# A small-head attention block with two feed-forward parts on one core: loads of the first batch reordered, set-up products moved, one-column products taken off the matrix engine

## The chip, the cores and the metric

The kernel runs on one core of a Trainium2 chip. The core has five instruction streams that run side by side and wait for each other through semaphores: TensorE (matrix products and transposes, written PE in the profile, with its weight loads apart as PEld), VectorE (DVE), ScalarE (ACT), GpSimd (POOL) and SyncE (SP), which here only issues DMA transfers. The metric is the device time of one execution in microseconds; lower is better. The kernel before was measured three times: 1343.65, 1344.02 and 1346.45 us, median 1344.02.

## The reference

The input is x with 8 batches of 512 tokens and 256 features, in float32 throughout. Each of four sub-layers normalises x without a gain (`_layernorm`) and adds its result to x. Cut to what matters:

```python
x = x + attn_a(layernorm(x))   # 16 heads of 16, rope, latent kv of 64, softmax with a distance decay
x = x + ffn(layernorm(x))      # 256 -> 1024 -> 256, relu
x = x + attn_b(layernorm(x))   # (q k^T * decay) v over 256 features, no softmax
x = x + ffn(layernorm(x))      # the same weights again
```

`attn_a` also adds 0.2 * sigmoid(q . mean(k)) * mean(v) for each head, through the output weights. `attn_b` has q = x Wq^T + bq and k = x Wk^T + bk. Its scores are therefore x (Wq^T Wk) x^T plus terms in which a bias meets a weight (Wq^T bk, Wk^T bq) and one number, the sum of bq * bk. These three terms, which depend on weights alone, are what the kernel calls bb; the weight product is ct.

## The kernel before, in words

**Tiling.** Tokens lie on the 128 partitions in NT = 4 tiles of a batch. The 16 heads of `attn_a` are worked in NG = 4 groups of 4, each head on its own 32 partitions, so that products of 32 rows stand side by side in the array. One item is a token tile and a pair of heads; there are 8 items to a group, 32 to a batch and 256 in all (NS).

**The pass over items.** `score_item` makes scores s for an item, VectorE takes their row maxima (`reduce_item`, tile mr). After the 8 items of a group, `shift` turns the maxima (mx), negates them (neg) and sends them by a DMA on ScalarE's queue into spare rows of qT. Then `prob_item` makes the transposed products t with the maxima already taken off, ScalarE exponentiates them (p), VectorE or GpSimd multiplies them by the decay table dec_a, and `pv_item` multiplies them by the values. Probabilities lag scores by LAG = 10 steps.

**The rest of a batch** (output weights, the two feed-forward parts, `attn_b`) is cut into units, which a planner slips between the steps. It keeps a clock of its own for each engine, with estimated costs written into each unit (`pe`, `then`), and takes a unit when its inputs are due and its credit allows. All of this is done while the program is built: on the chip each engine has one fixed order.

**The start, which the change touches.** It is written out by hand. `move` (line 90 of the profile) issues DMAs on SP's queue in program order. SP has eight semaphores for them and takes them in turn, so a DMA is issued only when the one eight places ahead of it has landed. The loads before are, in order: x of batch 0 in two halves, vec (all bias columns), wd (the latent weights), wk_in, wq_in, rope, wv, two rows, wqk_in (the `attn_b` weights), one column of vec into its lower 64 partitions, x of batch 1, dec_a, two one-row loads into the gates (ga), and bvc. Then `stripes` copies the rotated q and k from SBUF to SBUF into qT and kT, four DMAs to a group of heads, and `late_loads` brings the output weights, wvu, w1, w2, dec_b, and a unit brings x of batch 2.

TensorE starts with 14 products of the identity with itself (`warm`), transposes the normalised x (tr_a), gathers the q and k biases (`biases`, tile qk_bias), and makes the latent in two halves (`latent(0, 2)`, `latent(1, 2)`), q and k for both rotary halves (`projected`), and the values. `regroup_k` and `regroup_q` are ScalarE copies that bring wk_in and wq_in into the order of the heads. The latent's evacuation by ScalarE adds the column of vec and sums over tokens into lsum.

**Set-up products.** `plain(0)` and `plain(1)` transpose the two `attn_b` weights with TensorE, `product(0)` and `product(1)` make ct from them. `product_biases` makes bb with TensorE from one-column products. `mean_v` makes the mean of the values from lsum, also with one column. Before, `plain(0)` stands ahead of the first scores; `plain(1)` and the two products are slipped in after score steps 1, 3 and 5, and `product_biases` is a planner unit that may start at step 20:

```python
    between = {
        1: Unit(lambda: plain(1), 700, (("ACT", 600),)),
        3: Unit(lambda: product(0), 900),
        5: Unit(lambda: product(1), 900, (("ACT", 600),)),
        9: ga0,
    }
```

In the profile nearly everything that VectorE, ScalarE and GpSimd do carries line 69, the wrapper that pins their order; products carry line 200 (`mm`) and transposes line 203 (`flip`). Operations are therefore told apart by their tiles.

Of the kernel before, what the change touches and what calls it, by code (L numbers as in the profile page):

```python
# [9 lines left out]
F32 = mybir.dt.float32  # L10
AF = mybir.ActivationFunctionType
ALU = mybir.AluOpType
# [3 lines left out]
P = 128  # L16
B, T, D = 8, 512, 256
NH, HD = 16, 16
HH = 8
# [3 lines left out]
LAT = 64  # L23
# [12 lines left out]
def tile_kernel(  # L36
# [41 lines left out]
    fr = ctx.enter_context(tc.tile_pool(name="fr", bufs=1))  # L78
    at = ctx.enter_context(tc.tile_pool(name="at", bufs=2))
    rs = ctx.enter_context(tc.tile_pool(name="rs", bufs=2))  # L80
    ps_sc = ctx.enter_context(tc.tile_pool(name="ps_sc", bufs=2, space=PSUM))
    ps_pv = ctx.enter_context(tc.tile_pool(name="ps_pv", bufs=1, space=PSUM))
    ps_m = ctx.enter_context(tc.tile_pool(name="ps_m", bufs=3, space=PSUM))
# [5 lines left out]
    def move(to, src):  # L89
        tc.keep_in_program_order(nc.sync.dma_start(to, src))  # L90
# [6 lines left out]
    def resident(src, name, shape=None):  # L97
        t = const.tile(list(shape or src.shape), F32, tag=name, name=name)
        move(t, src)
        return t  # L100
# [2 lines left out]
        return const.tile(shape, F32, tag=name, name=name)  # L103

    xs = {0: xp.tile([P, NT, D], F32, tag="x", name="x_0")}
    for h in range(2):
        move(xs[0][:, 2 * h : 2 * h + 2, :], xv[0][:, 2 * h : 2 * h + 2, :])
    ident = keep([P, P], "ident")
    make_identity(nc, ident)
    half = keep([P, NT], "half")  # L110
    gps.memset(half, -0.5)
    vec = resident(vecs, "vec")

    wd_sb = keep([P, NC, 2, LAT], "wd_sb")
    for j in range(2):
        move(wd_sb[:, :, j, :], wdown)

    wk_in = at.tile([P, NH, 32], F32, tag="p", bufs=4, name="wk_in")
    for j in range(2):
        move(wk_in[j * LAT : (j + 1) * LAT].rearrange("p h d -> p (h d)"), wk[:, 0, :])  # L120
    wq_in = at.tile([P, NC, NH, 32], F32, tag="p", bufs=4, name="wq_in")
    move(wq_in.rearrange("p c h d -> p c (h d)"), wq[:, :, 0, :])

    rope_sb = keep([P, 2, T], "rope_sb")
    move(rope_sb, rope[0:HH].unsqueeze(0).to_broadcast([NH, HH, 2, T]))
# [6 lines left out]
    wqk_in = rs.tile([P, NC, 2, D], F32, tag="big", bufs=1, name="wqk_in")  # L132
    move(wqk_in, wb[:, :, 0:2, :])
    bv, b2 = row[:, 0, :], row[:, 1, :]
    move(vec[LAT:, V_BD : V_BD + 1], vecs[:LAT, V_BD : V_BD + 1])

# [62 lines left out]
    def mm(o, l, r, start=True, stop=True):  # L199
        tc.keep_in_program_order(nc.tensor.matmul(o, lhsT=l, rhs=r, start=start, stop=stop))  # L200
# [24 lines left out]

    def regroup_q(e):
        for c in range(NC):
            act.copy(wq_sb[:, c, e, :].rearrange("p (h d) -> p h d", d=HH), wq_in[:, c, :, e * HH : (e + 1) * HH])


    qk_bias = keep([P, 2, 2], "qk_bias")
# [10 lines left out]
    def biases():  # L242
        ps = misc("qk_bias")
        for g in range(NG):
            for j, v in enumerate((V_BQ, V_BK)):
                for e in range(2):
                    mm(ps[g * 32 : g * 32 + 32, 2 * j + e : 2 * j + e + 1], pick[:, e, :], vec[:, v + g : v + g + 1])
        act.copy(qk_bias.rearrange("p j e -> p (j e)"), ps[:, :4])
# [29 lines left out]
        if c == NC - 1:  # L278
            act.copy(ct.rearrange("p c d -> p (c d)"), ps)

    def product_biases():
        both = rs.tile([P, NC], F32, tag="ve", name="both")
        dve.tensor_mul(both, vec[:, V_BQB : V_BQB + NC], vec[:, V_BKB : V_BKB + NC])
        ones = rs.tile([P, P], F32, tag="xn", name="ones")
        gps.memset(ones, 1.0)
        ps = misc("bb")
        for j, v in ((0, V_BKB), (1, V_BQB)):
            for c in range(NC):
                for o in range(NC):
                    mm(  # L290
                        ps[:, 2 * j + c : 2 * j + c + 1], wr[j][:, o, c * P : (c + 1) * P], vec[:, v + o : v + o + 1],
                        o == 0, o == NC - 1,
                    )
        for o in range(NC):
            mm(ps[:, 4:5], ones, both[:, o : o + 1], o == 0, o == NC - 1)
        dve.tensor_copy(bb, ps[:, :5])
        dve.tensor_copy(wvu[:, :, D], bb[:, 2:4])


    class Unit:  # L300
# [55 lines left out]
    def front1(b):  # L356
        def latent(part=0, parts=1):
            if part == 0:
                lat_a[b] = fr.tile([P, T], F32, tag="lat", name=f"lat_{b}")
                lsum[b] = fr.tile([P, parts], F32, tag="lsum", bufs=1, name=f"lsum_{b}")  # L360
            ps = misc(f"lat_{b}_{part}")
            n = T // parts
            cols = slice(part * n, (part + 1) * n)
            for c in range(NC):
                mm(ps[:, :n], wd_sb[:, c].rearrange("p j n -> p (j n)"), xT_a[b]["xT"][:, c, cols], c == 0, c == NC - 1)
            act.activation(
                lat_a[b][:, cols], ps[:, :n], AF.Identity,
                bias=vec[:, V_BD : V_BD + 1], accum_out=lsum[b][:, part : part + 1],
            )


        def values():
# [14 lines left out]


        def mean_v():
            ps = misc(f"mv_{b}")  # L390
            n = lsum[b].shape[1]
            for c in range(NC):
                for j in range(n):
                    mm(ps[:, c : c + 1], wv_sb[:LAT, c * P : (c + 1) * P], lsum[b][:LAT, j : j + 1], j == 0, j == n - 1)
            m = fr.tile([P, NC], F32, tag="mv_a", name=f"mv_a_{b}")
            dve.scalar_tensor_tensor(m, ps[:, :NC], 0.1 / T, bvc, ALU.mult, ALU.add)
            for c in range(NC):
                gps.tensor_scalar(vmean[:, c, : NH + 1], vmask[:, c, :], m[:, c : c + 1], None, ALU.mult)

        def through_wo():  # L400
            ps = misc(f"me_{b}")
            for c in range(NC):
                mm(ps[:, :D], vmean[:, c, :], wo_sb[:, c, :], c == 0, c == NC - 1)
# [359 lines left out]
    gps.memset(vaug[0], 1.0)  # L763
    memory_buffers()
    picks()
    warm(14)
    regroup_k()
    n0[0].fn(), n1[0].fn()
    n0[1].fn(), n1[1].fn()
    n0[2].fn()  # L770
    biases()
    regroup_q(0)
    latent(0, 2)
    masks()
    dve.memset(qT[0], 0.0)
    gps.memset(kT[1], 1.0)
    gps.memset(qT[1], 0.0)
    gps.memset(vaug[1], 1.0)
    loads_before_scores()
    n1[2].fn()  # L780
    latent(1, 2)
    regroup_q(1)
    half_unit(0, 0, projected(0, 0))
    k_ps = [projected(1, e) for e in range(2)]
# [7 lines left out]
            stripes(j, g, e)  # L792
    late_loads()
    order0[1].fn()
    plain(0)
    gps.tensor_scalar(bvc, bvc, 0.1, None, ALU.mult)
    order0[0].fn()

# [129 lines left out]
        u.done = 0  # L928
    ga0.after = []
    mv0.step = 12  # L930
    chains = [[mv0, me0, Unit(product_biases, 2400, (("DVE", 500),), step=20)], setup]
    for b in range(1, B):
        ln0, u1 = front1(b)
        ln0[0].step = ln0[3].step = max(LAG, PER * (b - 1) + 2)
# [2 lines left out]
    for b in range(B):  # L937
# [3 lines left out]
    tail_work = sum(u.pe for u in chains[-1]) + sum(u.pe for u in chains[-2][26:])  # L941


    between = {
        1: Unit(lambda: plain(1), 700, (("ACT", 600),)),
        3: Unit(lambda: product(0), 900),
        5: Unit(lambda: product(1), 900, (("ACT", 600),)),
        9: ga0,
    }
    for t in range(LAG):  # L950
        step(t)
        if t in between:
# [161 lines left out]
```

## Time and profile before

| what | value |
|---|---|
| median of three executions | 1344.02 us (1343.65 to 1346.45) |
| the profiled execution's own time | 1346.04 us |
| its span, first to last instruction | 1344.3 us |
| mean granted TensorE clock | 0.97 |
| TensorE busy | 1262.7 us (94%), 6152 instructions |
| VectorE busy | 808.9 us (60%) |
| ScalarE busy | 451.8 us (34%) |
| GpSimd busy | 402.1 us (30%) |
| SP's DMA queue | 18502 packets, 22.71 MB |

A row of the timeline gives the start in us, the time from there to the end of the last of the instructions merged into it, the engine, the line, the operation, what it writes and reads with partitions x elements, and how many instructions there are; in brackets stands how long the engine had been idle before it, and what released it. A float32 product appears as two matrix instructions. A clock of 0.50 means that TensorE was granted half speed.

### The profile page before, as it was taken

The numbers are of one execution on the slowest core, as the hardware profiler recorded it, in microseconds if no ns is written. First come the engines' busy times: TensorE is split into PE (matmuls) and PEld (weight loads), VectorE is DVE, ScalarE is ACT, GpSimd is POOL, SyncE is SP. The second block draws the span as 40 slices with busy tenths as digits, with TensorE's granted clock in tenths as the row PEclk, the third lists the DMA queues.
The fourth block names the chain that finished last, engine by engine and source line by source line (L and its number), as shares of the span: only waits on it lengthen the run. The fifth ranks groups of instructions, "written<-read, shape, count | busy, mean of one in ns | idle before, by whom it ended". The sixth has DMA issues, their size and how long they took to land. (4 is left out here: it accounts for less than half of the span.)

```text
span 1344.3 us, 15699 instructions
## 1 busy us (share of the span) xinstructions
PE 1262.7 (94%) x6152; PEld 628.0 (47%) x6152; DVE 808.9 (60%) x1324; ACT 451.8 (34%) x649; POOL 402.1 (30%) x459
## 2 busy tenths in 40 slices
PE   6999888989899999999999999999999899999988
PEld 3333233534354554453444544544554445455665
DVE  5667976657656775658756666657755575343130
ACT  2234434333434334324334334333333333331201
POOL 4145443233412432314232324214321232222010
PEclk8779989989899999999999999999999999998999
DMA  4300010001000010001000100001000000000000
GB/s 132 118 17 17 1 49 1 1 9 41 1 17 0 19 31 1 1 15 50 1 1 1 44 22 1 1 9 41 1 1 3 14 1 1 1 16 0 0 16 16
DMA packets 19215, 23.96 MB, mean 18 GB/s; under 512 B 4139, under 2 KB 13740, under 8 KB 18862
## 3 DMA queue, kind: packets, MB, share of 16 engines
q1 hardware_dynamic: 18502, 22.71, 5.7%
q8 instruction: 48, 0.79, 0.2%
q10 hardware_dynamic: 640, 0.26, 0.1%
q14 instruction: 25, 0.20, 0.0%
HBM read 10.11 MB, written 4.19 MB: 11 GB/s over the span
## 5 line engine op out<-in xcount | busy, mean ns | idle before, releaser
L69 DVE TENSOR_REDUCE mr<-s 128x2 f32<-128x1024 f32 x256 | 312.4, 1222 | 256.6 <-PE t L200 240.6
L69 ACT ACTIVATE p<-t 128x1024 f32<-128x1024 f32 (+1 forms) x290 | 264.2, 924 | 532.7 <-PE t L200 488.4
L69 POOL TENSOR_TENSOR p<-p,dec_a 128x512 f32<-128x512 f32 x182 | 231.9, 1295 | 508.4 <-ACT p L69 495.7
L200 PE MATMUL s<-kT,qT 32*128 32x512 f32 x1024 | 294.9, 664 | 49.4 <-DVE mr L69 45.9
L200 PE MATMUL t<-qT,kT 32*128 32x512 f32 x1024 | 301.7, 658 | 2.0 <-DMA qT<-neg 1.7
L69 DVE TENSOR_TENSOR p<-p,dec_a 128x512 f32<-128x512 f32 x330 | 226.3, 727 | 20.8 <-ACT p L69 20.8
L200 PE MATMUL x<-w_sb,h_x 128*128 128x256 f32 x1024 | 233.9, 383 | 0.0
L200 PEld LDWEIGHTS x<-w_sb,h_x 128*128 128x128 f32 x1024 | 190.4, 190 | 54.8 <-issue 30.1
L200 PEld LDWEIGHTS s<-kT,qT 32*128 32x128 f32 x1024 | 79.5, 189 | 220.0 <-DVE mr L69 99.3
L200 PE MATMUL pv<-p,va 128*32 128x512 f32 x1024 | 149.7, 621 | 1.4 <-DVE p L69 1.0
L69 ACT ACTIVATE h_x<-hx,vec 128x512 f32<-128x512 f32 x128 | 88.0, 688 | 152.0 <-PE hx L200 152.0
L200 PE MATMUL hx<-xT_f,w_sb 128*128 128x512 f32 x256 | 120.2, 609 | 0.7 <-ACT xT_f L69 0.7
L200 PE MATMUL hx<-xT_g,w_sb 128*128 128x512 f32 x256 | 119.4, 608 | 0.7 <-ACT xT_g L69 0.7
L69 DVE TENSOR_TENSOR x<-x,x 128x256 f32<-128x256 f32 x64 | 27.1, 423 | 148.5 <-PE x L200 148.5
L200 PEld LDWEIGHTS t<-qT,kT 32*128 32x128 f32 x1024 | 81.9, 187 | 17.7 <-issue 9.5
L200 PEld LDWEIGHTS hx<-xT_g,w_sb 128*128 128x128 f32 x256 | 46.8, 193 | 63.6 <-issue 58.5
L200 PEld LDWEIGHTS hx<-xT_f,w_sb 128*128 128x128 f32 x256 | 46.4, 193 | 58.4 <-issue 51.7
L200 PEld LDWEIGHTS pv<-p,va 128*32 128x32 f32 x1024 | 22.9, 109 | 77.6 <-issue 40.8
L69 POOL TENSOR_TENSOR x<-x,row 128x256 f32<-128x256 f32 x64 | 48.1, 771 | 32.9 <-DVE xn_f L69 22.3
L69 POOL TENSOR_TENSOR rc<-rc,rs 128x512 f32<-128x512 f32 x30 | 39.4, 1335 | 12.4 <-DVE rs L69 12.4
L200 PE MATMUL bs<-xT_r,ret 128*128 128x512 f32 (+3 forms) x128 | 38.0, 441 | 0.0
L200 PE MATMUL bo<-ret 128*128 128x256 f32 x160 | 36.6, 382 | 0.0
(137 smaller groups left out, 1037.3 us busy)
## 6 DMA issues: line engine op xcount, KB each, us to landing
kT<-rc SPq DMA_DIRECT2D x64, 64.0 KB
out_dram<-x SPq DMA_DIRECT2D x32, 128.0 KB
qT<-rc SPq DMA_DIRECT2D x60, 64.0 KB
x<-in_x_dram SPq DMA_DIRECT2D x7, 512.0 KB
w_sb<-in_w_dram SPq DMA_DIRECT2D x2, 1024.0 KB
x<-in_x_dram SPq DMA_DIRECT2D x2, 256.0 KB
wq_in<-in_wq_dram SPq DMA_DIRECT2D x1, 512.0 KB
rope_sb<-in_rope_dram SPq DMA_DIRECT2D x1, 512.0 KB
```

The costliest lines, as they stand in the source:

```text
L69: ins = f(*a, **k)
L200: tc.keep_in_program_order(nc.tensor.matmul(o, lhsT=l, rhs=r, start=start, stop=stop))
```

## The change

All of it lies in the first of the eight batches, or in terms made once from the weights.

- Loads: the one-column load into vec stands right behind the load of vec; wq_in stands ahead of wk_in. The two halves of x are written as two calls instead of a loop, in the same order.
- Start of TensorE: 7 warm products, the qk biases, 6 warm products; both pairs of transposes together; both halves of the latent together, later. The first `regroup_q` is done by VectorE instead of ScalarE, behind `masks` and ahead of the clearing of qT.
- `plain(0)`, `plain(1)`, `product(0)`, `product(1)` all stand ahead of the first scores. In their places after score steps 1, 3, 5 and 7 stand two warm products each.
- `product_biases` goes. `bias_rows` copies the two bias vectors to a small DRAM tile with a DMA that writes single elements, and reads them back as rows spread over all partitions. `bias_products`, after score steps 0, 2 and 4, multiplies the weights by these rows on GpSimd and sums along them with ScalarE's accumulator.
- The two halves of lsum are added by GpSimd when a latent is made in two parts, so that `mean_v` uses one column.

```diff
     vec = resident(vecs, "vec")
+    move(vec[LAT:, V_BD : V_BD + 1], vecs[:LAT, V_BD : V_BD + 1])
...
+    wq_in = at.tile([P, NC, NH, 32], F32, tag="p", bufs=4, name="wq_in")
+    move(wq_in.rearrange("p c h d -> p c (h d)"), wq[:, :, 0, :])
     wk_in = at.tile([P, NH, 32], F32, tag="p", bufs=4, name="wk_in")
     for j in range(2):
         move(wk_in[j * LAT : (j + 1) * LAT].rearrange("p h d -> p (h d)"), wk[:, 0, :])
-    wq_in = at.tile([P, NC, NH, 32], F32, tag="p", bufs=4, name="wq_in")
-    move(wq_in.rearrange("p c h d -> p c (h d)"), wq[:, :, 0, :])
...
-    move(vec[LAT:, V_BD : V_BD + 1], vecs[:LAT, V_BD : V_BD + 1])
...
-            act.copy(wq_sb[:, c, e, :].rearrange("p (h d) -> p h d", d=HH), wq_in[:, c, :, e * HH : (e + 1) * HH])
+            (act.copy if e else dve.tensor_copy)(wq_sb[:, c, e, :].rearrange("p (h d) -> p h d", d=HH), wq_in[:, c, :, e * HH : (e + 1) * HH])
...
-    def product_biases():
...
+    b_row = dr.tile([2, D], F32, name="b_row")
+
+    def bias_rows():
+        move(b_row.rearrange("j (c p) -> p (j c)", p=P), vecs[:, V_BQB : V_BQB + 2 * NC])
+        wr["rows"] = at.tile([P, 4, D], F32, tag="p", bufs=4, name="b_rows")
+        move(wr["rows"][:, 0:2, :], b_row.unsqueeze(0).to_broadcast([P, 2, D]))
+
+    def bias_products(j):
+        b_rows = wr["rows"]
+        w = b_rows[:, 2:4, :]
+        if j == 2:
+            gps.tensor_tensor(w[:, 0, :], b_rows[:, 0, :], b_rows[:, 1, :], ALU.mult)
+            act.activation(w[:, 0, :], w[:, 0, :], AF.Identity, accum_out=bb[:, 4:5])
+            act.copy(wvu[:, :, D], bb[:, 2:4])
+            return
+        gps.tensor_tensor(w, wqk_in[:, :, j, :], b_rows[:, 1 - j, :].unsqueeze(1).to_broadcast([P, NC, D]), ALU.mult)
+        for c in range(NC):
+            act.activation(w[:, c, :], w[:, c, :], AF.Identity, accum_out=bb[:, 2 * j + c : 2 * j + c + 1])
...
+            if part == 1:
+                gps.tensor_add(lsum[b][:, 0:1], lsum[b][:, 0:1], lsum[b][:, 1:2])
...
-                for j in range(n):
-                    mm(ps[:, c : c + 1], wv_sb[:LAT, c * P : (c + 1) * P], lsum[b][:LAT, j : j + 1], j == 0, j == n - 1)
+                mm(ps[:, c : c + 1], wv_sb[:LAT, c * P : (c + 1) * P], lsum[b][:LAT, 0:1])
...
-    warm(14)
+    warm(7)
+    biases()
+    warm(6)
     regroup_k()
     n0[0].fn(), n1[0].fn()
     n0[1].fn(), n1[1].fn()
-    n0[2].fn()
-    biases()
+    n0[2].fn(), n1[2].fn()
+    masks()
     regroup_q(0)
-    latent(0, 2)
-    masks()
     dve.memset(qT[0], 0.0)
     gps.memset(kT[1], 1.0)
     gps.memset(qT[1], 0.0)
     gps.memset(vaug[1], 1.0)
+    bias_rows()
     loads_before_scores()
-    n1[2].fn()
-    latent(1, 2)
+    latent(0, 2), latent(1, 2)
     regroup_q(1)
...
-    plain(0)
+    plain(0), plain(1), product(0), product(1)
...
-    chains = [[mv0, me0, Unit(product_biases, 2400, (("DVE", 500),), step=20)], setup]
+    chains = [[mv0, me0], setup]
...
-    between = {
-        1: Unit(lambda: plain(1), 700, (("ACT", 600),)),
-        3: Unit(lambda: product(0), 900),
-        5: Unit(lambda: product(1), 900, (("ACT", 600),)),
-        9: ga0,
-    }
+    between = {t: Unit(lambda: warm(2), 500) for t in (1, 3, 5, 7)}
+    between[9] = ga0
+    for j, t in enumerate((0, 2, 4)):
+        between[t] = Unit(lambda j=j: bias_products(j), then=(("POOL", 1300), ("ACT", 1300)))
```

In the built program the order of each engine beyond the first batch is the same as before. Within it, the planner also puts the two k products of batch 1 ahead of the transposes of the first group's result (num).

More of the change, by code (lines that the diff above doesn't have):

```diff
@@ L80, in tile_kernel @@
     rs = ctx.enter_context(tc.tile_pool(name="rs", bufs=2))
+    dr = ctx.enter_context(tc.tile_pool(name="dr", bufs=1, space=bass.MemoryType.DRAM))
     ps_sc = ctx.enter_context(tc.tile_pool(name="ps_sc", bufs=2, space=PSUM))
@@ L105, in tile_kernel @@
     xs = {0: xp.tile([P, NT, D], F32, tag="x", name="x_0")}
-    for h in range(2):
-        move(xs[0][:, 2 * h : 2 * h + 2, :], xv[0][:, 2 * h : 2 * h + 2, :])
+    move(xs[0][:, 0:2, :], xv[0][:, 0:2, :])
+    move(xs[0][:, 2:4, :], xv[0][:, 2:4, :])
     ident = keep([P, P], "ident")
@@ L279, in product @@
             act.copy(ct.rearrange("p c d -> p (c d)"), ps)
-    def product_biases():
[L282 to L297, printed above, removed]
+    b_row = dr.tile([2, D], F32, name="b_row")
[14 more added lines that the diff above has]
+            act.activation(w[:, c, :], w[:, c, :], AF.Identity, accum_out=bb[:, 2 * j + c : 2 * j + c + 1])
     class Unit:
@@ L359, in latent @@
                 lat_a[b] = fr.tile([P, T], F32, tag="lat", name=f"lat_{b}")
-                lsum[b] = fr.tile([P, parts], F32, tag="lsum", bufs=1, name=f"lsum_{b}")
+                lsum[b] = fr.tile([P, 2], F32, tag="lsum", bufs=1, name=f"lsum_{b}")
             ps = misc(f"lat_{b}_{part}")
@@ L390, in mean_v @@
             ps = misc(f"mv_{b}")
-            n = lsum[b].shape[1]
             for c in range(NC):
-                for j in range(n):
-                    mm(ps[:, c : c + 1], wv_sb[:LAT, c * P : (c + 1) * P], lsum[b][:LAT, j : j + 1], j == 0, j == n - 1)
+                mm(ps[:, c : c + 1], wv_sb[:LAT, c * P : (c + 1) * P], lsum[b][:LAT, 0:1])
             m = fr.tile([P, NC], F32, tag="mv_a", name=f"mv_a_{b}")
```

## The prediction

> **What bounds the kernel now.** I read the page first. TensorE is busy 94% of the span and the chain that ended last is nearly all TensorE, so after the start the order of its instructions carries time through: a lead won early is kept. The edits end with the product biases at about 85 us, so I then asked for the work by stage and for the timeline of the first 100 us. By stage (window, its length, busy us and count of TensorE, weight loads, VectorE, ScalarE, GpSimd; then TensorE clock, DMA share, GB/s):
>
> ```profile
> 9.50:15.90 6.40, 0.00 (x0) 0.00 (x0) 0.73 (x1) 1.54 (x5) 3.06 (x3) 0.90 1.06 316
> 15.90:21.50 5.60, 5.59 (x10) 2.70 (x12) 0.01 (x1) 0.95 (x4) 0.00 (x0) 0.50 0.06 14
> 30.90:46.00 15.10, 14.36 (x49) 5.83 (x49) 9.47 (x9) 1.17 (x2) 0.00 (x0) 0.66 0.50 151
> 80.80:98.40 17.60, 16.80 (x72) 7.12 (x68) 10.82 (x17) 4.99 (x9) 5.93 (x5) 0.61 0.08 20
> ```
>
> TensorE does nothing for 6.4 us, then runs at half clock; the first scores (30.9 to 46) and the stage with the product biases (80.8 to 98.4) are slow as well. The timeline names the waits:
>
> ```profile
> 6.36 0.30 ACT L69 COPY wk_sb<-wk_in 64x128 f32<-64x128 f32 x1 [4.01 <-DMA wk_in<-in_wk_dram]
> 9.19 0.61 SPq L90 DMA_DIRECT2D vec<-in_vecs_dram  x1
> 14.82 0.47 ACT L69 ACTIVATE lat<-lat,vec 128x256 f32<-128x256 f32 x1 [4.63 <-DMA vec<-in_vecs_dram]
> 15.91 2.08 PE L200 MATMUL lat<-xT_a,wd_sb 128*128 128x256 f32 x4 [6.41 <-ACT xT_a L69]
> 26.26 1.73 SPq L90 DMA_DIRECT2D kT<-rc  x2
> 30.88 1.33 PE L200 MATMUL s<-kT,qT 32*128 32x512 f32 x8 [3.31 <-DMA qT<-rc]
> 51.94 1.93 PE L200 MATMUL t<-qT,kT 32*128 32x512 f32 x6 [1.71 <-DMA qT<-neg]
> 56.45 1.86 PE L200 MATMUL mv<-lsum,wv_sb 64*128 64x1 f32 x8
> 80.77 1.95 PE L200 MATMUL bb<-vec,wr 128*128 128x1 f32 x16
> 83.52 0.98 PE L200 MATMUL bb<-both,ones 128*128 128x1 f32 x4 [0.80 <-DVE both L69]
> ```
>
> ScalarE waits 4.63 us for the second `vec` load, issued at 9.19 behind the large loads; the second `xT_a` copy and TensorE stand behind it. The first scores wait for the stripes of qT, the first t products for `neg`; mv and bb are one-column products that take TensorE time.
>
> **What the Trainium skill says.** *TensorE: Matmul & The Clock Gate*, Part 1 (the HAM clock gate): the clock is halved after a window of about 3.4 us without work and comes back after a busy one. The trace agrees: idle from 9.5, half at 14.8, full at 21.5; half again from 31.7 to 41.9, 52.4 to 62.2 and 82.9 to 96.7. *DMA: Bandwidth & Descriptors*, "Two DMAs through the same engine are not ordered": a DMA that touches what another one writes is issued only when the first one's semaphore has come. In before, nothing on SP's queue shows such a wait, as `vec` had long landed.
>
> **Part 1, the load order.** The second `vec` load now stands right behind the first and writes into the same tile, so SP must wait for the first to land. That was issued at 1.73. Least: 2.1 us after issue, as the stripe issued at 28.72 that releases 30.88, so 3.9; most 5.5; I take 4.7, since 512 KB of x lies ahead and its second half was used at 4.40. SP's own durations then give: vec until 5.3 (0.61), wd until 6.6 (1.31), wq until 7.2 (0.60), wk until 8.4 (1.25); every load behind is about 2.9 us later than before. x's 512 KB took 3.7 us from issue (0.72 to 4.40), wq took 4.8 (4.88 to 9.69, with wk ahead), so wq lands at 10.3 to 11.4, taken 10.5. wk is now behind it: about 11.4 instead of 6.97. ScalarE still has the wk_sb copies ahead of both xT copies. That is the new wait: wk_sb done at 11.7, xT at 12.3 and 12.9 (0.59 each), latents from 12.4. Both latents and the first q cost 1.1 + 1.1 + 2.0 at full clock (end 16.6) and 2.1 + 2.1 + 3.6 at half (20.2). At TensorE's start the qk biases now wait for `vec` (3.9 to 4.7, between 7 and 6 warm products), so the transposes come at 7.8 instead of 6.22 and end near 8.8; the wait for wk hides that (uncovered, 1.6). From 8.8 TensorE is idle, so the clock is open; I take 18.5 against 21.49 before: 3.0 us won (1.3 to 4.9), not the 6.4 that the old wait shows. The q copies moved to VectorE (two at about 0.3) and the 1.76 us memset behind them end near 13, before VectorE has other work; uncovered they would cost 0.6.
>
> **Part 2, the stripes.** From the first q to the first stripe is 4.77 us of VectorE and GpSimd (21.49 to 26.26), unchanged but for the lsum addition on GpSimd (about 0.25, in its 12.4 us of idle): 23.3. SP must be free by then. Two DMAs are new ahead of x_1, dec_a, two ga and bvc: b_row (512 pieces of 4 bytes to HBM) and b_rows, which reads it back and so waits for it. The old loads up to wqk were in by about 13.7, now 16.2; no row shows such a DMA, so b_row lands between 17.5 and, by an estimate from the same page's 0.2 us average HBM latency ("Latency and other measured facts") with 32 pieces on each of 16 engines and none overlapped, 16.2 + 6.4 + 2.1 = 24.7. I take 18.5; issuing b_rows to bvc takes 0.6 + 0.6 + 0.3 + 0.6 + 0.4, so SP is free at 21.0 and hides it (at the upper bound the stripes are 3.9 us late).
>
> **Part 3, plain and product ahead of the scores.** Four transposes, twice, and four ct products now stand before the first score. Their last bank waits for VectorE's va additions, which end 8.5 us after the first q (21.49 to 29.95): 27.0. Four products at 0.52 end at 29.1; the stripes would have let scores start at 23.3 + 4.6 = 27.9. So 1.2 us is given back: start 29.1 against 30.88.
>
> **Part 4, the first scores.** Before, 30.88 to the mx flip at 45.92, 15.0 us at clock 0.66 with wr and ct (1.11 + 2.08 + 1.75) between. Now TensorE comes in warm, and four pairs of warm products (28 instructions in 4.83, so 0.69 a pair) replace them. VectorE's eight reductions at 1.2 bound it: 1.4 + 9.6 + 1.0 for the pairs = 12.0, so mx at 41.1, 4.8 us earlier. The bias products fall here: GpSimd 1.3 + 1.3 + 0.8 (rows of 128x512 at 1295 ns, 128x256 at 771), ScalarE five at about 0.66 (lat's 475 + 192 ns) and a copy, 3.5. Both were nearly idle in this stage (0.00 and 1.17 us). On ScalarE they stand ahead of `neg`; uncovered they cost up to 3.5.
>
> **Part 5, neg.** It took 5.4 us from issue (46.54) to t (51.94), while w1 and w2 filled the DMA engines until 51. Those loads move only with the stripes (3.0). By latency t comes at 41.7 + 5.4 = 47.1, by the loads' end at 48.9; I take 48.0: 3.9 us won of the 4.8.
>
> **Part 6, one-column products.** mv halves: 0.9 us. bb leaves TensorE: 80.77 to 84.50, 3.7 us, with VectorE idle. The clock fell at 82.9, in bb, and stayed low until 96.7; if it stays up VectorE is next: reduction, p, four rope operations and the division end at 86.8 instead of 90.14 (3.3 won), and by 98 about 6.6 is won. I take 5.0.
>
> **Sum.** 3.9 + 0.9 + 5.0 = 9.8 us. The profiled execution took 1346.04 (span 1344.3) and would take 1336.2; the median lies 2.0 lower, so 1344.02 - 9.8 = **1334.2 us**.
>
> **Rivals.** *Front gain lost* (0.18): wk lands later, or b_row holds the stripes by 3 us; only part 6 is left, 1338. For: both waits are new and unmeasured; against: the loads have slack of some 2 us before the stripes. *Clock kept* (0.15): TensorE doesn't cool before the latents and neg isn't held by the weights; 4.9 instead of 3.0, all of part 6 (7.5) and 2 more: 13 to 17 won, 1329. For: the idle of 3.6 us is about one window; against: neg's 5.4 us under load. *Nothing measurable* (0.08): the clock falls elsewhere near 85 and the front gives nothing: 1344. *Slower* (0.09): the HBM round trip. ScalarE's five sums, and so `neg`, stand behind it, and so do the stripes. To cancel part 6 the first stripe must be issued 6 us later than before, near 32, so b_row must land after about 29.5, 13 us after its turn (0.4 us for each piece in line); after 20 us it is about 1351. For: no row shows its price; against: `vec`'s 64 small pieces landed with the stream around them.
>
> **Numbers.** The likeliest case (0.50) is 1331 to 1338. From 1327 to 1341.5 holds all but the last two cases and an edge. Faster by over 0.2% 0.83, within 0.2% 0.08, slower 0.09; 0.2% (2.7 us) is about what this measurement can tell from no change.
>
> **What would show it.** After: wk_sb waits for wk_in until about 11.4, latents at 12.4; a gap on SP before the second vec; first stripe at 23.3, scores at 29, mx at 41, t at 48; clock near 1.0 in the scores and around 85. Wrong would be: SP waiting for b_row beyond 21, t still at 52, or a clock fall where bb was.

## The result and the profile after

The changed kernel takes 1337.08 us (median of four runs, 1335.86 to 1339.7) against 1343.84 for the kernel before (1343.29 to 1346.45). The ratio is 0.9949, with a 95% interval of 0.9928 to 0.9969: 6.9 us less. The forecast was 1334.2, and its likeliest case ran from 1331 to 1338. The time is in it, at its slow end, but it did not get there by the way foretold. Medians and ratios leave out executions in a second, slower state, which concerns one of e2's seven (2435.72 us).

| | profiled, before | profiled, after |
|---|---|---|
| own time, us | 1346.04 | 1339.7 |
| span, us | 1344.3 | 1337.9 |
| mean clock | 0.970 | 0.977 |
| TensorE busy, us | 1262.7 | 1256.9 |

The work of the changed kernel by stage (window, its length, busy us and count of TensorE, weight loads, VectorE, ScalarE, GpSimd; then TensorE clock, DMA share, GB/s):

```profile
3.40:6.80 3.40, 2.98 (x48) 2.79 (x46) 2.60 (x11) 0.16 (x1) 3.10 (x11) 1.00 0.12 31
...
9.50:15.15 5.65, 0.00 (x0) 0.00 (x1) 1.99 (x3) 1.23 (x4) 3.04 (x3) 0.65 1.03 244
...
18.50:24.00 5.50, 4.91 (x14) 1.64 (x13) 3.63 (x6) 0.95 (x4) 0.36 (x2) 1.00 0.00 0
31.90:44.20 12.30, 11.62 (x56) 4.88 (x57) 9.92 (x9) 4.60 (x17) 3.88 (x5) 1.00 0.33 89
44.20:51.60 7.40, 3.70 (x12) 0.98 (x8) 4.06 (x7) 0.59 (x1) 0.94 (x2) 1.00 1.00 379
52.40:62.20 9.80, 9.80 (x37) 3.06 (x34) 4.53 (x7) 3.36 (x6) 5.66 (x6) 0.50 0.04 13
80.80:98.40 17.60, 17.12 (x66) 5.22 (x66) 13.35 (x19) 6.95 (x16) 9.02 (x8) 0.90 0.12 31
```

The first scores (31.9 to 44.2) now run at full clock and the stage that held bb (80.8 to 98.4) at 0.90 instead of 0.61: the first as foretold, the second with one fall of the clock left. But the DMA engines stand nearly idle from 3.4 to 6.8 and wholly from 18.5 to 24 (the second stretch was idle before as well, with SP waiting for the rotation), and the stretch from `neg` to the first t (44.2 to 51.6) has grown to 7.4 us, half of it idle for TensorE. Then 9.8 us at half clock follow, as before. The timeline (start, length, engine, line, operation, tiles, count, and in brackets the idle time and what ended it):

```profile
1.72 3.77 SPq L91 DMA_DIRECT2D vec<-in_vecs_dram  x2
...
12.79 0.36 DVE L69 COPY wq_sb<-wq_in 128x128 f32<-128x128 f32 x2 [4.71 <-DMA wq_in<-in_wq_dram]
13.66 0.62 SPq L91 DMA_DIRECT2D b_row<-in_vecs_dram  x1
13.66 0.30 ACT L69 COPY wk_sb<-wk_in 64x128 f32<-64x128 f32 x1 [7.59 <-DMA wk_in<-in_wk_dram]
...
15.15 3.40 PE L201 MATMUL lat<-xT_a,wd_sb 128*128 128x256 f32 x8 [6.87 <-ACT xT_a L69]
...
22.61 0.34 SPq L91 DMA_DIRECT2D b_rows<-b_row  x1
...
25.84 1.68 SPq L91 DMA_DIRECT2D kT<-rc  x2
...
28.45 3.58 PE L201 MATMUL ct<-wr 128*128 128x256 f32 x8 [0.68 <-ACT wr L69]
...
31.96 1.14 PE L201 MATMUL s<-kT,qT 32*128 32x512 f32 x8
...
42.68 1.06 SPq L91 DMA_DIRECT2D w_sb<-in_w_dram  x2
...
44.20 1.12 ACTq L69 DMA_DIRECT2D qT<-neg  x1
...
51.62 1.61 PE L201 MATMUL t<-qT,kT 32*128 32x512 f32 x6 [3.72 <-DMA qT<-neg]
```

Two new waits are plain. ScalarE waits 7.59 us for wk_in, and TensorE 6.87 us for what ScalarE does behind it. SP issues b_row at 13.66 and nothing more until 22.61. The waits of SP's queue (what it waited for: us in total, times, longest) give the wait for b_row its price, and that for the first load of vec:

```profile
SPq L91 <- DMA b_row<-in_vecs_dram: 8.2, 1, 8.2
SPq L91 <- DMA vec<-in_vecs_dram: 2.7, 1, 2.7
```

In the kernel before the last three events of the start stand so on the timeline, with the loads of w1 and w2 (`w_sb`) first:

```profile
41.27 1.07 SPq L90 DMA_DIRECT2D w_sb<-in_w_dram  x2
...
46.54 1.11 ACTq L69 DMA_DIRECT2D qT<-neg  x1
51.94 1.93 PE L200 MATMUL t<-qT,kT 32*128 32x512 f32 x6 [1.71 <-DMA qT<-neg]
```

So `neg` leaves 2.3 us earlier than before (44.20 against 46.54), the loads of w1 and w2 leave 1.4 us later (42.68 against 41.27), and t comes where it came before: 51.62 against 51.94.

Where the time went, from the starts of the same instructions in both profiles: t leads by 0.3 us, me of batch 0 by 0.7 (62.59 against 63.31), the first q of batch 1 by 4.85 (94.64 against 99.49), the first aT by 6.4 (116.75 against 123.19). At the last hx products it is still 6.5 (1320.2 against 1326.7), so all of it is made before 117 us. From the first aT to the end both take the same 1221.1 us.

### The profile page after: what moved, and what is told of

The parts are those of the page before. It is cut to its first block, busy times and chain, and to the rows that moved or that the text cites. A ratio compares the mean times of both kernels' runs of the same rounds, so it can differ in the third digit from the quotient of the medians.

```text
span 1337.9 us, 15694 instructions
## 1 busy us (share of the span) xinstructions
PE 1256.9 (94%) x6142; PEld 626.7 (47%) x6142; DVE 809.6 (61%) x1323; ACT 453.6 (34%) x658; POOL 405.0 (30%) x462
## 2 busy tenths in 40 slices
DMA packets 19887, 24.23 MB, mean 18 GB/s; under 512 B 4683, under 2 KB 14284, under 8 KB 19534
## 5 line engine op out<-in xcount | busy, mean ns | idle before, releaser
L201 PE MATMUL wo<-wo_sb,aT 128*128 128x256 f32 x128 | 36.2, 405 | 0.5 <-ACT aT L69 0.5
```

## The experiments

Each ran beside the kernel before; 1343.9, 1342.94 and 1342.96 us were its medians in the three groups (e1 to e4, e5 to e8, e9 to e12). Ratios are to it; the ratio on record is not the quotient of the two medians, and the two differ by up to 0.0013. Gains in us with an interval are worked out from the ratio. In e2 to e8 and in e12 the two bias vectors lie as rows in the input data, so that one broadcast load fetches them and no trip is needed.

**e1: the front alone.** The changed kernel, with bb on TensorE again; the trip and its rows stay, unused.

```diff
-    def bias_products(j):
...
+    def product_biases():
...
-    chains = [[mv0, me0], setup]
+    chains = [[mv0, me0, Unit(product_biases, 2400, (("DVE", 500),), step=20)], setup]
...
-    for j, t in enumerate((0, 2, 4)):
-        between[t] = Unit(lambda j=j: bias_products(j), then=(("POOL", 1300), ("ACT", 1300)))
```

> Everything of the change stays, with the b_row round trip and its loads, but the product biases are made by TensorE again, at the old place. Theory A (all of the gain comes from bb leaving TensorE; the front gives nothing): first t near 51.6 as after the change, bb again about 3.7 us, the clock falls in it, and the time is that of before less 0.3 to 1 us: 1343, ratio 0.999 to 1.000. Rival B (the front carries a good part of the gain and bb's 4 us are given back later): 1340 or less, ratio 0.997 or less.

Measured: 1340.89 us, ratio 0.9974 (0.9963 to 0.9986), between the two forecasts; the interval reaches Rival B's 0.997 but not Theory A's 0.999. The starts of me of batch 0 and of the first q of batch 1, in the kernel before, the changed kernel and e1:

```profile
63.31 1.13 PE L200 MATMUL me<-wo_sb,vmean 128*128 128x256 f32 x4
99.49 1.98 PE L200 MATMUL q<-xT_a,wq_sb 128*128 128x512 f32 x4
```

```profile
62.59 1.13 PE L201 MATMUL me<-wo_sb,vmean 128*128 128x256 f32 x4
94.64 1.98 PE L201 MATMUL q<-xT_a,wq_sb 128*128 128x512 f32 x4
```

```profile
60.56 1.13 PE L201 MATMUL me<-wo_sb,vmean 128*128 128x256 f32 x4
96.74 1.98 PE L201 MATMUL q<-xT_a,wq_sb 128*128 128x512 f32 x4
```

From one to the other e1 takes 36.18 us, exactly what the kernel before takes; the changed kernel takes 32.05. By these profiles bb's share is 4.1 us. The front is not worth nothing: 3.5 us (1.9 to 5.0) with mv.

**e2: bb and mv alone.** The kernel before, with one column for mv and bb made by GpSimd and ScalarE after score steps 2, 4 and 6.

```diff
-    chains = [[mv0, me0, Unit(product_biases, 2400, (("DVE", 500),), step=20)], setup]
+    chains = [[mv0, me0], setup]
...
+    for j, t in enumerate((2, 4, 6)):
+        between[t] = Unit(lambda j=j: bias_products(j), then=(("POOL", 1300), ("ACT", 1300)))
```

> The kernel before, with nothing but the one-column products changed: mv from one column, bb by GpSimd and ScalarE after score steps 2, 4 and 6. The two bias vectors come as rows in one load from the laid-out inputs, so there is no round trip through HBM. Theory A: all of the gain, first t near 52, no clock fall where bb was, 1337 to 1338.5, ratio 0.995 to 0.996. Rival B: half of it, 1341, ratio 0.998.

Measured: 1339.07 us, ratio 0.9957 (0.9938 to 0.9975), 5.8 us less by the ratio and 4.8 by the medians. The first q of batch 1 comes at 96.67, 2.8 us earlier than before although t was 1.1 us later (53.01). The ratio by itself is the one that Theory A named. The gains of e1 and e2 add up to more (9.3) than the changed kernel has (6.9), within their intervals; mv's shorter products are in both. Theory A (all from bb) falls in its strict form, by e1. That bb is the larger part is the likelier reading, but the intervals of the two gains overlap.

**e3: no trip.** The changed kernel, with one load of the rows in place of b_row and b_rows.

```diff
-        move(b_row.rearrange("j (c p) -> p (j c)", p=P), vecs[:, V_BQB : V_BQB + 2 * NC])
...
-        move(wr["rows"][:, 0:2, :], b_row.unsqueeze(0).to_broadcast([P, 2, D]))
+        move(wr["rows"][:, 0:2, :].rearrange("p j d -> p (j d)"), rows[3 * D : 5 * D].partition_broadcast(P))
```

> The changed kernel without the round trip: the bias rows come in one load from the laid-out inputs; all else as changed. SP no longer waits 8.2 us. Theory C (the trip alone lost the front gain): stripes from 25 at full pace, first scores at 29.5 instead of 31.96, first t 2.5 us earlier, 1334.5. Rival D (the first scores wait as much for ct, which ended at 32.03, and the first t for the end of the weights' loads): scores still at 31 to 32, first t 1 to 1.5 us earlier as SP is done earlier, 1335.5 to 1336.5.

Measured: 1334.75 us, ratio 0.9931 (0.9911 to 0.9950), which overlaps that of the changed kernel; the profiled execution (1338.59) was the slowest of six. Its timeline shows why taking an 8.2 us wait away won so little:

```profile
26.10 1.72 SPq L90 DMA_DIRECT2D kT<-rc  x2
...
29.41 1.99 PE L200 MATMUL ct<-wr 128*128 128x256 f32 x8 [0.68 <-ACT wr L69]
...
31.34 1.14 PE L200 MATMUL s<-kT,qT 32*128 32x512 f32 x8
```

The first stripe leaves at 26.10, no earlier than with the trip (25.84): q starts at 18.33, as late as before the edit, and SP now waits 8.3 us for the rotation instead of b_row. The time is the one that Theory C (the trip alone) named, but not its way: the scores start at 31.34 and t is 1.0 us earlier (50.58), which is what Rival D said.

**e4: the weight products back among the scores.** e3 with `plain(1)`, `product(0)` and `product(1)` after score steps 1, 3 and 5 and no warm pairs.

```diff
-    plain(0), plain(1), product(0), product(1)
+    plain(0)
...
-    between = {t: Unit(lambda: warm(2), 500) for t in (1, 3, 5, 7)}
-    between[9] = ga0
+    between = {
+        1: Unit(lambda: plain(1), 700, (("ACT", 600),)),
+        3: Unit(lambda: product(0), 900),
+        5: Unit(lambda: product(1), 900, (("ACT", 600),)),
+        9: ga0,
+    }
```

> As the run without the round trip, but plain(1) and the two ct products stand among the scores again, where they were before the change, in place of the warm products. Rival D: first scores 2 us earlier than with ct ahead (29.5), but the scores take 13 to 15 us instead of 11.6, so mx comes no earlier (43 to 44) and the time is the same within 1 us. Theory C: no difference in the first scores.

Measured: 1337.32 us, ratio 0.9944 (0.9928 to 0.9961), not separated from e3, though its median is 2.6 us above. The scores start at 29.60, waiting for a stripe, but take 15.4 us to mx (44.98), at a mean clock of 0.67, instead of 11.6; mx is 2.0 us later than in e3, and t comes at 51.17 against 50.58. What the place of the products gives at one end of the scores it takes at the other, and t hardly moves either way. That is the way of Rival D; whether its time (within 1 us of e3) holds, the intervals can't tell.

**e5: wk first.** e3 with wk_in ahead of wq_in, as in the kernel before.

```diff
-    move(wq_in.rearrange("p c h d -> p c (h d)"), wq[:, :, 0, :])
...
     for j in range(2):
         move(wk_in[j * LAT : (j + 1) * LAT].rearrange("p h d -> p (h d)"), wk[:, 0, :])
...
+    move(wq_in.rearrange("p c h d -> p c (h d)"), wq[:, :, 0, :])
```

> This is e3 (no round trip) with the key weights loaded ahead of the query weights again, as in the kernel before. Theory W (the late key weights hold the latents in the changed kernel and that is what reaches the first t): wk_sb comes at about 9 us instead of 13.7, the latents start at about 10 to 11 instead of 14.75 and the first q at about 13 to 15 (it now waits for the query weights, about 12.8), the first stripe is issued at about 22 instead of 26.1, first scores at about 27, and the first t at 47 to 48 instead of 50.6, since the loads of w1 and w2 move with the stripes: 1331 to 1333 against 1334.75 for e3. Rival X (the wait only changes its name: the query weights, the rope and the clock then bind): latents earlier, but q at 17 to 18, first stripe at 25 or later, t at 50 and 1334 to 1335.

Measured: 1331.54 us, ratio 0.9912 (0.9899 to 0.9925).

```profile
10.89 1.99 PE L200 MATMUL lat<-xT_a,wd_sb 128*128 128x256 f32 x8 [0.74 <-ACT xT_a L69]
...
20.60 1.72 SPq L90 DMA_DIRECT2D kT<-rc  x2
...
44.51 2.10 PE L200 MATMUL t<-qT,kT 32*128 32x512 f32 x6 [2.73 <-DMA qT<-neg]
```

With q at 13.79 and the first scores at 25.84 this is Theory W, at each step as early as expected or earlier.

**e6: the vec column later.** e5 with the one-column load behind wk_in.

```diff
-    move(vec[LAT:, V_BD : V_BD + 1], vecs[:LAT, V_BD : V_BD + 1])
...
         move(wk_in[j * LAT : (j + 1) * LAT].rearrange("p h d -> p (h d)"), wk[:, 0, :])
+    move(vec[LAT:, V_BD : V_BD + 1], vecs[:LAT, V_BD : V_BD + 1])
```

> This is e5 with the one-column load of vec behind the key weights, so that SP no longer waits 2.7 us for the first load of vec. Theory V (this wait delays every later load): all loads behind are issued 2.7 us earlier, wk_sb at about 7.5, query weights about 10, the first q at about 11 to 13, the first stripe at about 20, t at about 45 to 46, and about 2 us less time than e5. Rival Y: the loads share the bandwidth, so what is issued earlier lands no earlier by more than 1 us, or the column itself is then late and holds the latents and the bias of q; time within 1 us of e5.

Measured: 1329.28 us, ratio 0.9889 (0.9873 to 0.9906). The wait is gone, and the timeline reads:

```profile
8.25 1.99 PE L200 MATMUL lat<-xT_a,wd_sb 128*128 128x256 f32 x8
...
18.81 1.71 SPq L90 DMA_DIRECT2D kT<-rc  x2
...
22.13 3.57 PE L200 MATMUL ct<-wr 128*128 128x256 f32 x8 [0.68 <-ACT wr L69]
25.63 1.14 PE L200 MATMUL s<-kT,qT 32*128 32x512 f32 x8
```

The latents come 2.6 us earlier than in e5 and the stripe 1.8, but the scores only 0.2: ct stands ahead of them and fell into a stretch of half clock (3.57 us against 1.99 in e5). t is 0.9 us earlier (43.57). The step from e5 alone isn't separated by the intervals; from e3 to e6, both load edits together, it is.

**e9: the trip kept, the load order mended.** The changed kernel with the load order of e6.

```diff
-    move(vec[LAT:, V_BD : V_BD + 1], vecs[:LAT, V_BD : V_BD + 1])
...
-    move(wq_in.rearrange("p c h d -> p c (h d)"), wq[:, :, 0, :])
...
         move(wk_in[j * LAT : (j + 1) * LAT].rearrange("p h d -> p (h d)"), wk[:, 0, :])
+    move(vec[LAT:, V_BD : V_BD + 1], vecs[:LAT, V_BD : V_BD + 1])
...
+    move(wq_in.rearrange("p c h d -> p c (h d)"), wq[:, :, 0, :])
```

> This is the changed kernel with the trip through HBM kept, and only the load order of e6: key weights ahead of the query weights, the one-column load of vec behind the key weights. Theory L (the two new waits in the loads cost the changed kernel its front gain, with or without the trip): the trip starts 3 us earlier with the loads, b_row is issued at about 10 to 11 and lands at about 19, its rows at about 25, the stripes go out from about 20.5 to 22, first scores at 26 to 27, first t at 45 to 46, and 1330 to 1332 against 1337.1 for the changed kernel. Rival T (the trip binds the stripes as soon as the loads are mended, so it is what decides): SP stays held to 22 or later, first scores at 29 or later, t at 48 or later, 1333 to 1336.

Measured: 1336.83 us, ratio 0.9955 (0.9944 to 0.9967): nothing won on the changed kernel. SP's waits, the timeline and a stretch of the scores:

```profile
SPq L91 <- DMA b_row<-in_vecs_dram: 9.5, 1, 9.5
```

```profile
20.05 0.34 SPq L91 DMA_DIRECT2D b_rows<-b_row  x1
...
22.91 3.68 PE L201 MATMUL ct<-wr 128*128 128x256 f32 x8 [0.67 <-ACT wr L69]
23.16 1.82 SPq L91 DMA_DIRECT2D kT<-rc  x2
...
29.18 1.53 PE L201 MATMUL s<-kT,qT 32*128 32x512 f32 x8 [2.58 <-DMA qT<-rc]
```

```profile
34.20:37.60 3.40, 3.40 (x16) 1.68 (x12) 2.28 (x2) 0.59 (x3) 0.11 (x1) 0.50 0.41 104
```

q now starts at 12.78 instead of 18.39, 5.6 us earlier, but SP sits on b_row until 20.05, the x, dec_a, ga and bvc loads go after it, and the stripes after those. The scores wait for a stripe, the clock falls, and mx comes at 43.58, where the changed kernel has it (43.59). That is Rival T, though b_row landed 2 us sooner than it said. Together with e3 and e6 this makes a square:

| | load order of the change | load order of e6 |
|---|---|---|
| with the trip | 1337.08, ratio 0.9949 (first scores 31.96) | 1336.83, 0.9955 (29.18) |
| without the trip | 1334.75, 0.9931 (31.34) | 1329.28, 0.9889 (25.63) |

The late weights and the trip stand side by side ahead of the same stripes. Either alone holds the scores; removing one wins 2.3 us at most, removing both wins 7.8, and only e6's interval stands apart from the other three.

**e10: w1 and w2 early, on the kernel before.** The only edit:

```diff
         move(bvc, rows[0:D].rearrange("(c p) -> p c", p=P))
+        late["w1"] = resident(w1, "w1_sb")
+        late["w2"] = resident(w2, "w2_sb")
...
-        late["w1"] = resident(w1, "w1_sb")
-        late["w2"] = resident(w2, "w2_sb")
```

> This is the kernel before with one edit: w1 and w2 (2 MB) issued behind bvc, ahead of the stripes. Theory N (these loads fill the DMA engines while neg's 8 KB are on the way): from the issue of neg to the first t about 3.5 us instead of 5.4, so t about 2 us earlier than 51.9 and the time 1.5 to 2 us below the kernel before. Rival Q (the stripes, behind 2 MB on the same queue, come later): first scores at 32 or later instead of 30.9, and a time equal or longer.

Measured: 1337.89 us, ratio 0.9971 (0.9959 to 0.9983): 3.9 us less by the ratio, 5.1 by the medians. From `neg` to t it takes 2.6 us, and TensorE is at work all the while:

```profile
48.17 1.12 ACTq L69 DMA_DIRECT2D qT<-neg  x1
...
50.75 0.70 PE L200 MATMUL t<-qT,kT 32*128 32x512 f32 x2
```

The first scores came at 31.98, as Rival Q had it, so t is only 1.2 us earlier than before; yet me of batch 0 is 4.9 earlier (58.38 against 63.31). The rest is the clock. The same stretch of both kernels, before first:

```profile
52.40:62.20 9.80, 9.80 (x40) 3.87 (x34) 4.47 (x7) 3.37 (x6) 4.28 (x5) 0.50 0.00 0
```

```profile
52.40:62.20 9.80, 9.06 (x52) 3.94 (x50) 9.43 (x14) 5.08 (x10) 5.62 (x6) 1.00 0.01 3
```

Without the idle time ahead of t the clock doesn't fall: 52 products instead of 40 in 9.8 us. From t to me takes 7.6 us here and 11.4 in the kernel before. The wait for `neg` was paid twice, once as idle time and, for 3.8 us, as half clock behind it. The other profiles say the same. In the five without idle time ahead of t (e7, e8, e10, e11, e12) it is 7.6 us from t to me; in the other nine, with 1.7 to 3.7 us of idle time, it is 9.7 to 11.4.

**e7: w1 and w2 early, on e6.** The edit of e10.

> This is e6 with the loads of w1 and w2 (2 MB) issued on SP's queue ahead of the stripes, right behind bvc, instead of behind the first stripes. Theory N (neg takes 7.4 us because these loads fill the DMA engines): from the issue of neg to the first t 2.5 to 3.5 us instead of 7.4, so t about 4 us earlier after mx. Rival Q (the stripes then stand in line behind 2 MB, about 11 us at 190 GB/s): the first scores come 5 us or more later than in e6, at the end t is no earlier or later, and the time is 0 to 5 us above e6.

Measured: 1325.1 us, ratio 0.9858 (0.9840 to 0.9875), the fastest kernel of the study, 18 to 19 us below the kernel before and 12 below the changed one. Its interval just overlaps that of e6.

```profile
37.12 1.12 ACTq L69 DMA_DIRECT2D qT<-neg  x1
...
40.83 1.15 PE L200 MATMUL t<-qT,kT 32*128 32x512 f32 x6
```

```profile
37.60:41.00 3.40, 3.39 (x13) 1.15 (x14) 2.49 (x7) 0.59 (x1) 0.83 (x2) 1.00 0.54 184
```

From `neg` to t 3.7 us instead of 5.7 in e6 (37.87 to 43.57), TensorE busy all the while and the clock at 1.00; from t to me 7.6. The stripes lose nothing (scores at 24.88), because the 2 MB fill a stretch in which e6 leaves the DMA engines more than half idle (share 0.39 and 0.35 from 17.0 to 20.4 and 23.8, against 1.05 and 0.83). Theory N holds, though 3.7 us is a little over the 2.5 to 3.5 expected, and Rival Q falls here.

**e8: the products back, on e7.** The edit of e4.

> This is e7 with plain(1) and both weight products among the first scores again, in the places of the warm pairs. If the stripes bind the first scores in e7 (Rival Q), the products ahead of the scores cost nothing there and moving them back makes this kernel 2 to 4 us slower than e7; if the products bind (Theory D: first scores stand right behind ct), the scores start 2 to 3.5 us earlier, and take 3 us longer, so that the time is within 1.5 us of e7.

Measured: 1328.58 us, ratio 0.9884 (0.9865 to 0.9903). The scores start at 25.22, waiting for a stripe, and take 15.6 us (mx 40.80), at a mean clock of 0.64, instead of 11.6: 3.5 us slower than e7, in Rival Q's range, though the two intervals overlap a little.

**e11: the trip back, on e7.** The edit of e3 turned round: b_row and b_rows in place of the one load.

> This is e7 with the trip through HBM put back, which shows the price of the trip where the other waits are gone, with w1 and w2 then issued behind the rows that are read back. Theory T: SP is held for b_row some 8 us, w1 and w2 leave at about 24 and fill the engines in front of and beside the stripes, so first scores at 28 to 30 instead of 24.9 and t at 45 to 47 instead of 40.8: 1329 to 1332 against 1325.1. Rival (the trip is covered by the latents and the rotation, as the prediction had it): within 1.5 us of e7.

Measured: 1338.7 us, ratio 0.9966 (0.9953 to 0.9980), 14 us slower than e7.

```profile
19.92 0.34 SPq L91 DMA_DIRECT2D b_rows<-b_row  x1
...
22.82 1.65 SPq L91 DMA_DIRECT2D w_sb<-in_w_dram  x2
25.29 2.18 SPq L91 DMA_DIRECT2D kT<-rc  x2
...
33.88 2.09 PE L201 MATMUL s<-kT,qT 32*128 32x512 f32 x8 [9.67 <-DMA qT<-rc]
```

w1 and w2 now leave right ahead of the stripes, and TensorE waits 9.67 us for a stripe behind them. Worse than Theory T: the trip doesn't only delay, it throws the large loads onto the stripes. Its 22 executions spread from 1333.45 to 1344.37, and the profiled one took 1334.88, so the profiles of e7 and e11 differ by about 10 us and not by 14; what makes the spread stays open.

**e12: no warm pairs, on e7.**

```diff
-    between = {t: Unit(lambda: warm(2), 500) for t in (1, 3, 5, 7)}
-    between[9] = ga0
+    between = {9: ga0}
```

> This is e7 without the four pairs of warm products among the first scores. The prediction priced the pairs at 1.0 us in this stage. If they only fill TensorE's waits for VectorE's reductions, removing them gains nothing: first scores to mx stays at 11.6 us, and t and time within 1 us of e7. If they stand in the way, mx comes 1 us earlier and the time is 1 us less. If they hold the clock up, the clock falls in the scores, and the scores, the t and the time are 2 us or more later than in e7.

Measured: 1328.97 us, ratio 0.9909 (0.9888 to 0.9931), 4 us slower than e7 and with an interval apart from e7's. The same stretch of the scores, e7 first, then e12:

```profile
30.80:34.20 3.40, 3.40 (x18) 1.42 (x16) 2.83 (x4) 1.50 (x7) 0.93 (x2) 1.00 0.27 77
```

```profile
30.80:34.20 3.40, 3.21 (x12) 1.01 (x8) 2.36 (x2) 0.79 (x5) 0.60 (x1) 0.50 0.21 67
```

The third branch came: without the pairs the clock falls and the scores take 13.7 us (23.93 to 37.66) instead of 11.6, and t is 2.2 us later (43.05). The pairs cost nothing that shows here; they hold the clock. The two profiled executions hide it in their totals (1324.55 and 1324.85): e12 is 1.6 us behind at the first aT (105.78 against 104.16) and wins most of that back behind it.

## Why the prediction was right or wrong

The sum was 3.9 (t earlier) + 0.9 (mv) + 5.0 (bb) = 9.8 us. The two profiled executions differ by 6.3. By the starts of their instructions the front and mv together gave 0.7, bb 4.1 and a stretch of half clock that is gone 1.6. That the time lies in the likeliest case is in part luck: the last 1.6 us stand in no term of the sum, and without them the time would, as an estimate, be near 1339, outside that case.

| step | predicted | measured |
|---|---|---|
| Part 1: SP's wait for the first vec; vec issued until | 5.3 | 5.49 |
| wq in use | 10.5 | 12.79 |
| wk in use (second half) | 11.4 | 14.19 (first half 13.66) |
| latents | 12.4 | 15.15 |
| first rotation after q | 18.5 | 20.37 |
| Part 2: b_row landed | 18.5 (17.5 to 24.7) | 22.6 |
| first stripe | 23.3 | 25.84 |
| Part 3: four ct products | 2.1 long | 3.58 |
| first scores | 29.1 | 31.96 |
| Part 4: first scores to mx | 12.0 long | 11.6 |
| mx | 41.1 | 43.59 |
| Part 5: `neg` issued to t | 6.3 long (5.4 to 7.2) | 7.4 |
| t | 48.0 | 51.62 |
| Part 6: mv | 0.9 won | 0.85 (1.86 to 1.01 long) |
| bb | 5.0 won | 4.1 |

**Part 1: mechanism right, size wrong.** SP did wait for the first vec, 2.7 us. With the second vec's own issue behind it the loads moved by 3.3 us (wd from 2.23 to 5.54), and wk behind wq became the new wait. The term mis-sized is wq's landing. It was given 3.9 us from issue and took 5.9 (6.85 to 12.79). During SP's wait the DMA engines ran dry (share 0.12 from 3.4 to 6.8, against 0.64 in the kernel before); from 9.5 to 15.15 they were full. Why wq took longer than the 4.8 us of the kernel before the records don't show. At 15.15 the clock, left open, had fallen (half from 11.2), and both latents took 3.40 us. Won: 1.1 us at the first rotation instead of 3.0. e5 and e6 show the term on the kernel without the trip: with wk first again and the column behind it, the latents come at 8.25.

**Part 2: the choice inside the bounds failed.** b_row took 8.95 us from issue, near the upper bound rather than the lower; 18.5 was chosen because other work seemed to hide it. At the upper bound the prediction had the stripes 3.9 us late; they were 2.5 late. The estimate rested on the Trainium skill, *DMA: Bandwidth & Descriptors*, "Latency and other measured facts", 0.2 us on average. That its upper end, with nothing overlapped (6.4 + 2.1 = 8.5 us), comes near the 8.95 measured is luck. By the DMA records the small packets pass between 16.5 and 18.4 us, in under 2 us instead of 6.4; the rest is 2.8 us ahead of them, while earlier loads fill the engines, and 4.2 us behind them in which no packet is recorded. In "Rules for kernel authors" the same page says that a strided last dimension becomes one descriptor for each element, and advises against it. b_row is such a DMA: the changed kernel has 527 more packets under 512 B than e3, which lacks it (4683 against 4156).

**Part 3: right in its first term, wrong in the clock.** ct started at 28.45, 1.4 after the 27.0 foretold, and lasted 3.58 instead of 2.1, as the clock was 0.50 from 28.3 to 31.7. What made it fall isn't shown: e3 has the same short gaps ahead of ct (0.68 us) and ran ct at full clock, in 1.99 us. The scores stand right behind ct. The stripe of qT that they also need left at 29.62; with the 2.2 us that the kernel before shows for it (28.72 to 30.88) it landed, as an estimate, near 31.8, so both bind.

**Part 4: right in length, wrong in the reason for one term.** 11.6 us against 12.0, at full clock, with bb's work on GpSimd and ScalarE from 34.48 to 40.05, hidden ahead of `neg` as foretold. The 1.0 us put down for the pairs is wrong in sign: in e7 and e12 they are worth 2.1 us of this stage.

**Part 5 failed, and most of the front's gain with it.** "Those loads move only with the stripes (3.0)" was the step. They moved 1.4 us the other way, since the first stripe left only 0.4 us earlier and SP then waited between stripes for b_rows, x and dec_a (0.5, 1.0 and 0.6 us). t is released by `neg`, and `neg` waits out w1 and w2: 2.3 us earlier at mx became 0.3 at t. The rival *Front gain lost* named the mechanism, wk later and b_row holding the stripes, and its 1338 is nearer to 1337.08 than the forecast. *Clock kept* named `neg` held by the weights as the thing to be freed; e7 and e10 freed it, and it was worth more than its 2 us (3.9 in e10).

**Part 6: right.** bb's place gave 4.1 of 5.0. The clock did fall once more in that stage (86.3 to 89.7, 3.4 us instead of the 13.7 of before), which can account for the 0.9 missing but isn't shown to. The 1.6 us behind it, a fall from 110.3 to 113.7 that is gone, isn't bb's: e1 has bb on TensorE and lacks the fall too (from the first q of batch 1 to aT 22.1 us in e1 and in the changed kernel, 23.7 before).

**A reading that doesn't hold.** The prediction says that the trace of the kernel before agrees with the page on the clock. It does at the start (idle from 9.5, half from 14.7, full from 21.5) and at 31.7, behind an idle time of 3.31 us. It does not at 52.4, where TensorE had waited 1.71 us, nor at 82.9, in the middle of bb's products.

**What stays open.** In the profile the front gives 0.7 us with mv. In e1, which has the same front, me of batch 0 leads by 2.75 us, and its time says 1.9 to 5.0; the changed kernel less e2 gives about 1. So the front's own gain isn't settled better than about 1 to 3.5 us, and e1's interval reaches further. bb's share depends on the clock too: the stretch that gave 4.1 us takes 34.5 us in e10, which keeps bb on TensorE, and 32.0 to 33.9 in the eleven kernels without it. And from the first aT on, TensorE has the same 5681 instructions in all fourteen profiles, yet that part takes from 1217.3 us (e12) to 1221.2 (e11). The early edits thus move the end by up to 4 us in a way that nothing here foretells; the part's mean clock of 0.98 or 0.99 points to where half-clock stretches fall. The new order of TensorE's start, the q copies on VectorE and the shorter mv were never run by themselves.

## What to carry to other kernels

Ask of each wait that an edit removes which other wait stands beside it ahead of the same instruction: two waits of about 8 us here gave 2 us at most when one was removed and 8 when both were. A small transfer with work queued behind it (here `neg`, 8 KB) was late with large loads in flight, and the idle time on the matrix engine was paid again in clock behind it; send large loads into a stretch where the DMA engines have nothing to do. The DMA of many single elements was a long latency here, though its packets passed quickly, and it blocks everything that stands behind its reader on the same queue.

## What the runs showed of the hardware

- 512 pieces of 4 bytes to HBM took 8.95 us from issue until the dependent load could be issued, and 10.2 in e9 (9.85 to 20.05). The small packets themselves passed between 16.5 and 18.4 us in the changed kernel and between 14.0 and 15.4 in e9, behind loads issued earlier. After the last of them 4.2 and 4.7 us went by with no DMA packet on record (share 0.00 from 18.5 to 24.0 in the changed kernel). What fills that time the records don't show.
- 8 KB on ScalarE's queue took 7.4 us to its consumer while 2 MB from SP's queue kept the engines busy (share 1.00, 379 GB/s), and at most 2.6 us where they had come earlier (e10; TensorE did not wait for it there). The Trainium skill (*DMA: Bandwidth & Descriptors*, "Queues, rings and completion order") has each engine take turns between queues by packet; that does not mean that a small transfer goes through at once.
- The Trainium skill (*TensorE: Matmul & The Clock Gate*, Part 1) says that about 3.4 us of sustained work brings the clock back. From 52.4 to 62.2 TensorE was recorded busy for 9.80 of 9.80 us and had half clock throughout, in the changed kernel and in the one before; in e12 it was busy for 3.21 of 3.40 us at half clock. At the start of the changed kernel the page does fit: work from 15.15, full clock from about 18.0. So being recorded as busy is not enough to bring the clock back, and here the measurement decides. The ends of products are modelled in this profile, so it can't tell how busy the array itself was.
